# First image's attention: half of the fp16 casts by a converting DMA, and VectorE's other work dealt out one item at a time

## The chip, the cores and the metric

The kernel runs on one core of a Trainium2 chip. A core has a matrix engine (TensorE, PE in the profile, with a row PEld for its weight loads), a vector engine (VectorE, DVE), a scalar engine (ScalarE, ACT), a general engine (GpSimd, POOL), a sync engine (SyncE, SP) that here issues most transfers, and 16 DMA engines that move data. Matrix results land in PSUM, everything else on the core lies in SBUF. Each engine works through its own list of instructions in order, and waits on semaphores for the others.

The metric is the device time of one execution in microseconds; lower is better. The kernel before takes 2591.39 us, the median of three runs (2590.61 to 2596.2).

## What is computed

Two attention layers, one after the other, over x of shape (8, 512, 32, 32): eight images, 512 channels, 1024 positions. The first layer has eight heads of 64 channels and rounds q, k and v to 256 levels; the second has one head of 512 channels. The change touches the first layer's attention only:

```python
def _L0_conv_ref(x, gn_w, gn_b, qkv_w, qkv_b, proj_w, proj_b):
    h = group_norm(x.reshape(b, c, T), gn_w, gn_b)
    qkv = jnp.einsum('oc,bct->bot', qkv_w, h) + qkv_b[None, :, None]
    q, k, v = jnp.split(qkv.reshape(b * NUM_HEADS, -1, T), 3, axis=1)
    q, k, v = fake_quant(q), fake_quant(k), fake_quant(v)
    scale = 1.0 / math.sqrt(math.sqrt(ch))
    w = jnp.einsum('bct,bcs->bts', q * scale, k * scale)
    w = jax.nn.softmax(w, axis=-1)
    a = jnp.einsum('bts,bcs->bct', w, v)
    a = jnp.einsum('oc,bct->bot', proj_w, a) + proj_b[None, :, None]
    return xf + a
...
x = _L0_conv_ref(x, ...)
x = _L1_conv_ref(x, ...)   # group norm, one head of 512 channels, projection, residual
```

## The kernel before

**Stages.** A first phase (to about 590 us) normalises all images and makes q, k and v, which go to DRAM. Then comes the first layer's attention of image 0 (590 to 703 us), interleaved with `fold()`, which multiplies weights of the second layer together. Then two groups of image 1's attention are issued ahead (`LEAD = 2`), image 0 is projected (from 726 us), and from there the second layer of one image and the first layer's attention of the next run side by side to the end.

**Units.** The attention's heads go in pairs (`j`, 0 to 3), the queries in two halves (`hf`) of 512, the keys in eight tiles of 128 (`s`, 0 to 7). One key tile of one half of one pair of one image is a *unit* `u`; an image has 64. A unit goes through these steps:

1. `scores(u)` (line 982): PE makes `st` = k'q for both heads, 128 keys x 2 x 512; ACT takes the exponential to `pt`, fp32, 128x1024 (0.52 MB). `ptp` has four such buffers. On every second unit of image 0, `next(folding)` puts one more product of `fold` ahead of the scores.
2. `split(u)` (line 1010): `pt` is cut into two fp16 tiles whose sum is precise enough: `two[:, 0]` is `pt` cast to fp16 (`cast`), `two[:, 1]` is `pt - two[:, 0]` (`rest`, always on DVE). `partp` has six such buffers. In image 0, units with `s % 4 == 3` are `plain`: they stay fp32, in `aside`, and are not split.
3. `over_keys` (line 1043): PE adds v times both halves to `av`. `totals` (line 1068): PE adds up the exponentials themselves in `sm`.
4. `finish(b, j, hf)` (line 1084), after a half's last unit: ACT copies `av` to `ao` and `sm` to `rs`. After a pair's second half, SP gathers the sums into `apart`; `spread` (DVE) adds and inverts them, writes them to DRAM (`rs_d`), and two transfers broadcast them back into `rs`; `divide` (DVE) multiplies `ao` by `rs`. `rs` has one buffer, which the next pair needs.

Which engine casts, in the kernel before: units with `s % 4 == 2` GpSimd; in image 0 and in the two groups issued ahead, `s == 5` VectorE; all others ScalarE.

**Order of PE's work.** The loop in `attention()` goes by four units. For image 0 (`dense`), with `u` a multiple of four: scores of `u+6`, `u+7`; `over_keys` and `totals` of `u`, `u+1`; split of `u+6`, `u+7`; scores of `u+8`, `u+9`; `over_keys` and `totals` of `u+2`, `u+3`; `finish` after a half's last group; split of `u+8`, `u+9`. At a pair's first group, `load_pair` (line 917) fetches the next pair's q and k into `raw` (two buffers, SP), DVE quantises each (`quant`, `quant2`), and `fetch_v` fetches v into the buffer that comes free and quantises it, with a second copy for the plain tiles (`whole`).

**Who sets the order on the other engines.** `InOrder` wraps DVE, ACT and PE. `dve.later(name, cost, work, ready, within)` and `settle(name)` are a planner for the later images (`InOrder.planned = True`): work is kept in a list with its cost and due time, and put between other work. For image 0 and the two groups issued ahead `planned` is False: `later` runs the work at once, and the framework's scheduler places the instructions of each engine by their dependences. So there each quantisation is issued where `load_pair` stands, and `spread` and `divide` where `finish` stands.

Of the kernel before, what the change touches and what calls it, by code (L numbers as in the profile page):

```python
# [25 lines left out]
PAIRS = HEADS // 2  # L26
# [32 lines left out]
def attn_pair_kernel(  # L59
# [9 lines left out]
    nc = tc.nc  # L69
    PSUM = bass.MemoryType.PSUM  # L70

    class InOrder:
# [73 lines left out]
        def settle(self, what):  # L146

            while True:
                i = next((i for i, c in enumerate(self.chores) if c[0] == what), None)
                if i is None:  # L150
                    return
                self.begin(i)
# [3 lines left out]
    def elements(n):  # L156

        return 0.21 + n * 0.957e-3
# [147 lines left out]
    with ExitStack() as fast:  # L306
# [605 lines left out]
        def plain(b, s):  # L912
            return b == 0 and s % 4 == 3

        ao = {}

        def load_pair(b, j):

            nm = f"{b}_{j}"
            raws = []  # L920

            def fetch(i, src):
                if (b, j, i) == (0, 0, 2):
                    raw = aop.tile([P, NH, 512], F32, tag="ao", name="raw_first").rearrange(
                        "p h n -> p (h n)"
                    )
                else:
                    raw = raw_p.tile([P, T], F32, tag="raw", name=f"raw_{nm}_{i}")
                nc.sync.dma_start(
                    raw if i < 2 else raw.rearrange("p (t d) -> p t d", t=NT), src  # L930
                )
                raws.append(raw)

            def whole(raw, _, i):
                quant2(raw.rearrange("p (t d) -> p t d", t=NT)[:, 3::4, :], vfs[j], i)

            fetch(0, q_d[b][j])
            fetch(1, k_d[b][j])
            qt = qkp.tile([P, T], BF, tag="q", name=f"q_{nm}")
            kt = qkp.tile([P, T], BF, tag="k", name=f"k_{nm}")  # L940
            vt = qkp.tile([P, NT, P], F16, tag="v", name=f"v_{nm}")
            todo = (qt, kt, vt.rearrange("p t d -> p (t d)"))

            if b == 0:
                vfs[j] = xp.tile([P, 2, 256], F32, tag="x", name=f"vf_{nm}")[:, :, 0:P]

            def quants(i):
                for step in (quant, quant2, *([whole] if i == 2 and b == 0 else [])):
                    dve.later(
                        "qk" if i < 2 else "qv", 0.7, lambda step=step: step(raws[i], todo[i], i),  # L950
                        pe.t + 12.0, 45.0,
                    )

            def fetch_v():
                if len(raws) == 2:
                    fetch(2, v_d[b][:, :, bass.ts(j, P)])
                quants(2)

            if (b, j) == (0, 0):
                fetch(2, v_d[b][:, :, bass.ts(j, P)])  # L960
            quants(0)
            quants(1)
            dve.later("qk", 0.0, fetch_v)
            return qt, kt, vt

        settle = dve.settle

        def attention():

# [4 lines left out]
                     for s in range(NT)]  # L974
            pairs = {}
            pairs[0, 0] = load_pair(0, 0)
            pts, parts, avs, sms, rss, ready = {}, {}, {}, {}, {}, {}
            st_free, at_hand = [0.0, 0.0], set()

            aside = l2p.tile([P, 3, NT // 2, 256], F32, tag="vsum", name="aside")  # L980
# [29 lines left out]
            def split(u):  # L1010

                b, j, hf, s = units[u]
                pt, there = pts.pop(u)
                if plain(b, s):
                    parts[u], ready[u] = pt, there
                    return
                two = partp.tile([P, 2, 2, 512], F16, tag="two", name=f"two_{b}_{j}_{hf}_{s}")
                parts[u] = two

                def rest():  # L1020
                    dve.tensor_tensor(two[:, 1], pt, two[:, 0], ALU.subtract)
                    ready[u] = dve.t

                def cast(copy=act.copy):
                    at_hand.add(u)
                    copy(two[:, 0], pt)  # L1026
                    done_at = act.t if copy == act.copy else there + 1.5
                    dve.later("sum", elements(1024), rest, done_at + 0.1, 9.0)

                if s % 4 == 2:  # L1030
                    cast(nc.gpsimd.tensor_copy)
                elif not InOrder.planned and s == 5:
                    cast(dve.tensor_copy)
                else:
                    act.later("cast", 1.02, cast, there, 7.0)

            def need(u):

                while u not in ready:
                    e, name = (act, "cast") if u not in at_hand else (dve, "sum")  # L1040
                    e.begin(next(i for i, c in enumerate(e.chores) if c[0] == name))
# [39 lines left out]
                            mm(row, lhsT=ones16, rhs=two[:, n // 2, n % 2, :], start=(s == 0),  # L1081
                               stop=(s == NT - 1 - (b == 0 and n > 1)))

            def finish(b, j, hf):

                nm = f"{b}_{j}"
                if hf == 0:
                    settle("ao")
                    ao[b, j] = aop.tile([P, NH, 512], F32, tag="ao", name=f"ao_{nm}")
                    rss[b, j] = l1p.tile([P, NH, 512], F32, tag="rs", name=f"rs_{nm}")  # L1090
                aot, rs = ao[b, j], rss[b, j]
                act.do(0.6, lambda: act.copy(aot[:, hf, :], avs.pop((b, j, hf))))
                act.do(0.6, lambda: act.copy(rs[:, hf, :], sms.pop((b, j, hf))))
                if hf == 0:
                    return
                del rss[b, j]
                n = b * PAIRS + j

                apart = small.tile([P, 2, 16], F32, tag="apart", name=f"apart_{nm}")
                for w in range(2):  # L1100
                    nc.sync.dma_start(
                        apart[:, w, :],
                        rs[2 * w * QUAD : 2 * (w + 1) * QUAD : QUAD].rearrange(
                            "r h (p k) -> r h p k", k=16
                        ),
                    )

                def divide():
                    dve.scalar_tensor_tensor(aot, aot, scl[:, 2:3], rs, ALU.mult, ALU.mult)

                def spread():
                    r = rcs[:, n * 16 : (n + 1) * 16]
                    dve.tensor_add(r, apart[:, 0, :], apart[:, 1, :])
                    dve.reciprocal(r, r)
                    nc.sync.dma_start(rs_d[n].rearrange("r (p k) -> (r p) k", k=16), r)
                    for i, r in enumerate(HALF):
                        nc.sync.dma_start(
                            rs[r], rs_d[n][2 * i : 2 * i + 2, :].partition_broadcast(CH)
                        )
                    dve.later("ao", elements(1100), divide, dve.t + 7.0, 20.0)  # L1120

                dve.later("ao", 0.4, spread, pe.t + 5.0, 8.0)

            for u in (0, 2, 4):
                for i in (u, u + 1):
# [3 lines left out]
            for u in range(0, len(units), 4):  # L1129
                b, j, hf, s = units[u]  # L1130
                if hf == 0 and s == 0:
                    n = b * PAIRS + j + 1
                    if n < B * PAIRS:
                        pairs[divmod(n, PAIRS)] = load_pair(*divmod(n, PAIRS))
                    settle("qv")

                def two(what, v):  # L1140
                    if v < len(units):
                        what(v)
                        what(v + 1)

                pe.t += 0.12
                if not late:
                    two(scores, u + 6)
                if late:
                    over_keys((u, u + 1))
                    two(scores, u + 6)  # L1150
                    totals((u, u + 1))
                    over_keys((u + 2, u + 3))
                    totals((u + 2, u + 3))
                    two(split, u + 6)
                    two(scores, u + 8)
                elif dense:
                    over_keys((u, u + 1))
                    totals((u, u + 1))
                    two(split, u + 6)
                    two(scores, u + 8)  # L1160
                    over_keys((u + 2, u + 3))
                    totals((u + 2, u + 3))
                else:
                    over_keys(range(u, u + 4))
                    totals(range(u, u + 4))
                    two(split, u + 6)
                    two(scores, u + 8)
                if s == NT - 4:
                    finish(b, j, hf)
                two(split, u + 8)  # L1170
                pe.t += 0.15
                last = (j, hf, s) == (PAIRS - 1, NH - 1, NT - 4)
                yield b + last
# [989 lines left out]
```

## Time and profile before

| what | before |
|---|---|
| median of three runs | 2591.39 us (2590.61 to 2596.2) |
| the profiled execution's own time | 2596.26 us |
| its span, first to last instruction | 2594.5 us |
| mean granted clock of PE | 0.994 |
| POOL's casts, whole span | 128, 1338 ns mean, 171.3 us |
| DVE's subtractions, whole span | 496, 1235 ns mean, 604.3 us |
| ACT's casts, whole span | 358, 1056 ns mean, 362.6 us |
| image 0's attention, 590 to 703 us: PE, DVE, ACT, POOL busy | 106.48, 100.29, 101.16, 21.00 us |
| the same: DMA share, GB/s | 0.36, 116 |

The profile is of one execution, so its durations add up to its own time, 2596.26 us, and not to the median. Busy times are sums over instructions; a wait is the idle time of an engine ahead of an instruction, with what ended it. The last two rows belong to a window: a stretch of the span with the busy time of every engine inside it, the clock granted to PE and the mean busy share of the 16 DMA engines.

### The profile page before, as it was taken

To read this page: it belongs to the slowest core of one execution; us is meant where nothing else is said; L and a number is where in the kernel's file an instruction comes from. 1 tells how busy PE (TensorE), PEld (TensorE's weight loads), DVE (VectorE), ACT (ScalarE), POOL (GpSimd) and SP (SyncE) were. 2 spreads that over 40 slices of the span, in tenths; PEclk is the share of its full clock that TensorE was granted. 3 is DMA by queue.
4 is the path that set the end of the run, shared out by engine and by line. 5 is a ranking of instruction groups with operands and counts; after the bars stand their busy time and mean duration, and the time that the engine had idled before them with its cause. 6 is when DMAs were issued, how large, how long until landed. Compare 5 with 4: busy or idle time off the path is not lost.

```text
span 2594.5 us, 38713 instructions
## 1 busy us (share of the span) xinstructions
PE 2535.6 (98%) x15670; PEld 1754.2 (68%) x15670; DVE 1905.8 (73%) x2748; ACT 1360.4 (52%) x1696; POOL 193.8 (7%) x153
## 2 busy tenths in 40 slices
PE   7999999999989999999999999999999999999998
PEld 4788888873237765775677577757766775777687
DVE  6788777669867777777877787778777777775544
ACT  3222222218856674666566566647665765664121
POOL 0000000001110001000100011010001000100000
PEclk9899999999999999999999999999999999999999
DMA  4343333334311232223212332231232123212211
GB/s 167 130 148 139 115 119 118 129 126 135 115 50 54 58 111 102 66 78 111 87 56 70 125 99 58 94 107 63 85 107 98 46 79 122 83 51 84 86 37 38
DMA packets 156014, 243.09 MB, mean 94 GB/s; under 512 B 26545, under 2 KB 93105, under 8 KB 154289
## 3 DMA queue, kind: packets, MB, share of 16 engines
q1 hardware_dynamic: 125264, 182.81, 21.3%
q10 hardware_dynamic: 30560, 57.71, 6.5%
q8 instruction: 125, 2.05, 0.3%
q14 instruction: 65, 0.52, 0.1%
HBM read 153.64 MB, written 86.28 MB: 92 GB/s over the span
## 4 chain that ended last, share of the span: by engine, by line
PE 84%; DVE 5%; ACT 2%; issue 2%; DMA 2%; POOL 0%; SPq 0%; ACTq 0%; DVEq 0%
PE s L208 15%; PE o L208 14%; PE qkps L208 12%; PE pj L208 9%; PE av L208 7%; PE v2ps L208 7%; PE g L208 7%; PE vps L208 6%; PE st L208 4%; PE sm L208 3%; DVE two L91 2%; ACT pt L91 1%; DMA rs<-rs_d 0%; DVE acc L91 0%; DVE h L91 0%
## 5 line engine op out<-in xcount | busy, mean ns | idle before, releaser
L91 ACT ACTIVATE pt<-st,esc 128x1024 f32<-128x1024 f32 x496 | 528.6, 1115 | 348.7 <-PE st L208 326.2
L91 DVE TENSOR_TENSOR two<-pt,two 128x1024 f16<-128x1024 f32 x496 | 604.3, 1235 | 129.2 <-POOL two L1026 106.9
L91 ACT CAST two<-pt 128x1024 f16<-128x1024 f32 x358 | 362.6, 1056 | 5.3 <-ACT p L91 5.1
L1026 POOL CAST two<-pt 128x1024 f16<-128x1024 f32 x128 | 171.3, 1338 | 1537.3 <-ACT pt L91 771.5
L208 PE MATMUL av<-two,v 128*32 128x512 f16 x3968 | 244.7, 381 | 0.2
L208 PE MATMUL s<-g,h 128*128 128x256 f32 x1024 | 233.4, 380 | 0.0
L208 PE MATMUL pj<-ao,wp 128*128 128x512 f32 x512 | 223.8, 595 | 0.0
L208 PEld LDWEIGHTS s<-g,h 128*128 128x128 f32 x1024 | 192.9, 190 | 31.0 <-issue 4.3
L91 ACT ACTIVATE u_ring<-qkps,qkbt 128x512 f32<-128x512 f32 x89 | 61.1, 687 | 252.6 <-PE qkps L208 220.3
L208 PE MATMUL st<-q,k 64*128 64x512 bf16 x1024 | 165.8, 383 | 17.6 <-ACT pt L91 12.6
L208 PEld LDWEIGHTS <-v 128*32 128x32 f16 x3968 | 91.3, 96 | 134.0 <-issue 60.7
L208 PE MATMUL s<-g,sums 128*128 128x256 f32 x768 | 178.4, 381 | 0.2 <-DVE p L91 0.2
L208 PEld LDWEIGHTS pj<-ao,wp 128*128 128x128 f32 x512 | 96.0, 190 | 121.6 <-issue 111.1
L208 PE MATMUL o<-p,v 128*128 128x256 f32 x768 | 175.2, 382 | 1.0 <-DVE p L91 1.0
L208 PEld LDWEIGHTS o<-p,v 128*128 128x128 f32 x768 | 144.3, 190 | 27.1 <-issue 5.7
L208 PEld LDWEIGHTS s<-g,sums 128*128 128x128 f32 x768 | 144.7, 190 | 24.2 <-issue 4.1
L208 PEld LDWEIGHTS <-k 64*128 64x128 bf16 x1024 | 35.6, 94 | 156.6 <-issue 155.0
L208 PE MATMUL sm<-two,ones 128*32 128x512 f16 x1984 | 136.1, 379 | 1.9 <-ACT rs L91 1.9
L208 PE MATMUL qkps<-half,w_high 128*128 128x512 f32 x480 | 134.3, 402 | 0.0
L208 PE MATMUL qkps<-half,w_low 128*128 128x512 f32 x480 | 132.3, 398 | 1.9 <-DVE half L91 1.9
L208 PE MATMUL qkps<-half,w_mix 128*128 128x512 f32 x480 | 132.5, 398 | 0.6 <-DVE half L91 0.6
L208 PE MATMUL g<-h,wa 128*128 128x256 f32 x512 | 122.0, 387 | 2.7 <-DVE h L91 2.5
(219 smaller groups left out, 3838.3 us busy)
## 6 DMA issues: line engine op xcount, KB each, us to landing
rs<-rs_d SPq DMA_DIRECT2D x80, 256.0 KB
x<-in_x_dram SPq DMA_DIRECT2D x32, 512.0 KB
q_d<-wa SPq DMA_DIRECT2D x32, 512.0 KB
k_d<-wa SPq DMA_DIRECT2D x32, 512.0 KB
v_d<-v_ring SPq DMA_DIRECT2D x32, 512.0 KB
raw<-q_d SPq DMA_DIRECT2D x32, 512.0 KB
raw<-k_d SPq DMA_DIRECT2D x32, 512.0 KB
x_d<-h SPq DMA_DIRECT2D x64, 256.0 KB
```

What stands on the lines that cost most here:

```text
L91: ins = self.latest = op(*args, **kw).ins
L208: ins = nc.tensor.matmul(ps, lhsT=lhsT, rhs=rhs, **kw).ins
L1026: copy(two[:, 0], pt)
```

## The change

Three parts, all inside the first layer's attention:

- **Casts by DMA.** In image 0 units with `s` in `CAST_BY_DMA = (1, 2, 5, 6)` are cast by `nc.gpsimd.dma_start(two[:, 0], pt)`: a transfer from SBUF to SBUF that reads fp32 and writes fp16, issued by GpSimd. That is 32 transfers. Before, `s` = 1 was ACT's, `s` = 5 DVE's and `s` = 2 and 6 GpSimd's. Units with `s` = 0 and 4 stay on ACT.
- **The subtraction is put off.** For these units `rest` is kept in `put_off` and issued at the split of the unit two later, or when `need(u)` asks for it.
- **Dealing.** In the unplanned part, quantisations, `fetch_v`, `spread` and `divide` go into a list, `dealt`, each with the unit from which it may run (`u + 10` for q, k, `fetch_v` and `spread`, `u + 15` for `divide`, `u + 18` for v, counted from the group at which they are put in). Each split issues at most one of them (`deal`); `settle` issues what has the asked name.

With the branch for `s == 5` gone, units 69 and 77 (image 1, in the groups issued ahead) are cast by ACT instead of DVE.

```diff
--- before.py
+++ after.py
@@ -912,9 +912,26 @@
         def plain(b, s):
             return b == 0 and s % 4 == 3
 
+
+        dealt = []
+
+        def deal(u):
+            i = next((i for i, (at, *_) in enumerate(dealt) if at <= u), None)
+            if i is not None:
+                dealt.pop(i)[2]()
+
+        def settle(what):
+            while True:
+                i = next((i for i, (_, name, _) in enumerate(dealt) if name == what), None)
+                if i is None:
+                    break
+                dealt.pop(i)[2]()
+            dve.settle(what)
+
         ao = {}
-
-        def load_pair(b, j):
+        CAST_BY_DMA = (1, 2, 5, 6)
+
+        def load_pair(b, j, u=None):
 
             nm = f"{b}_{j}"
             raws = []
@@ -946,10 +963,11 @@
 
             def quants(i):
                 for step in (quant, quant2, *([whole] if i == 2 and b == 0 else [])):
-                    dve.later(
-                        "qk" if i < 2 else "qv", 0.7, lambda step=step: step(raws[i], todo[i], i),
-                        pe.t + 12.0, 45.0,
-                    )
+                    name, work = "qk" if i < 2 else "qv", lambda step=step: step(raws[i], todo[i], i)
+                    if u is None or InOrder.planned:
+                        dve.later(name, 0.7, work, pe.t + 12.0, 45.0)
+                    else:
+                        dealt.append((u + (10 if i < 2 else 18), name, work))
 
             def fetch_v():
                 if len(raws) == 2:
@@ -960,10 +978,12 @@
                 fetch(2, v_d[b][:, :, bass.ts(j, P)])
             quants(0)
             quants(1)
-            dve.later("qk", 0.0, fetch_v)
+            if u is None or InOrder.planned:
+                dve.later("qk", 0.0, fetch_v)
+            else:
+                dealt.append((u + 10, "qk", fetch_v))
             return qt, kt, vt
 
-        settle = dve.settle
 
         def attention():
 
@@ -974,7 +994,7 @@
                      for s in range(NT)]
             pairs = {}
             pairs[0, 0] = load_pair(0, 0)
-            pts, parts, avs, sms, rss, ready = {}, {}, {}, {}, {}, {}
+            pts, parts, avs, sms, rss, ready, put_off = {}, {}, {}, {}, {}, {}, {}
             st_free, at_hand = [0.0, 0.0], set()
 
             aside = l2p.tile([P, 3, NT // 2, 256], F32, tag="vsum", name="aside")
@@ -1011,6 +1031,10 @@
 
                 b, j, hf, s = units[u]
                 pt, there = pts.pop(u)
+                if not InOrder.planned:
+                    for v in [v for v in put_off if v < u - 1]:
+                        put_off.pop(v)()
+                    deal(u)
                 if plain(b, s):
                     parts[u], ready[u] = pt, there
                     return
@@ -1021,6 +1045,11 @@
                     dve.tensor_tensor(two[:, 1], pt, two[:, 0], ALU.subtract)
                     ready[u] = dve.t
 
+                if b == 0 and s in CAST_BY_DMA:
+                    nc.gpsimd.dma_start(two[:, 0], pt)
+                    put_off[u] = rest
+                    return
+
                 def cast(copy=act.copy):
                     at_hand.add(u)
                     copy(two[:, 0], pt)
@@ -1029,13 +1058,13 @@
 
                 if s % 4 == 2:
                     cast(nc.gpsimd.tensor_copy)
-                elif not InOrder.planned and s == 5:
-                    cast(dve.tensor_copy)
                 else:
                     act.later("cast", 1.02, cast, there, 7.0)
 
             def need(u):
 
+                if u in put_off:
+                    put_off.pop(u)()
                 while u not in ready:
                     e, name = (act, "cast") if u not in at_hand else (dve, "sum")
                     e.begin(next(i for i, c in enumerate(e.chores) if c[0] == name))
@@ -1081,7 +1110,7 @@
                             mm(row, lhsT=ones16, rhs=two[:, n // 2, n % 2, :], start=(s == 0),
                                stop=(s == NT - 1 - (b == 0 and n > 1)))
 
-            def finish(b, j, hf):
+            def finish(b, j, hf, u):
 
                 nm = f"{b}_{j}"
                 if hf == 0:
@@ -1117,9 +1146,15 @@
                         nc.sync.dma_start(
                             rs[r], rs_d[n][2 * i : 2 * i + 2, :].partition_broadcast(CH)
                         )
-                    dve.later("ao", elements(1100), divide, dve.t + 7.0, 20.0)
-
-                dve.later("ao", 0.4, spread, pe.t + 5.0, 8.0)
+                    if InOrder.planned:
+                        dve.later("ao", elements(1100), divide, dve.t + 7.0, 20.0)
+                    else:
+                        dealt.append((u + 15, "ao", divide))
+
+                if InOrder.planned:
+                    dve.later("ao", 0.4, spread, pe.t + 5.0, 8.0)
+                else:
+                    dealt.append((u + 10, "ao", spread))
 
             for u in (0, 2, 4):
                 for i in (u, u + 1):
@@ -1131,7 +1166,7 @@
                 if hf == 0 and s == 0:
                     n = b * PAIRS + j + 1
                     if n < B * PAIRS:
-                        pairs[divmod(n, PAIRS)] = load_pair(*divmod(n, PAIRS))
+                        pairs[divmod(n, PAIRS)] = load_pair(*divmod(n, PAIRS), u)
                     settle("qv")
 
 
@@ -1166,7 +1201,7 @@
                     two(split, u + 6)
                     two(scores, u + 8)
                 if s == NT - 4:
-                    finish(b, j, hf)
+                    finish(b, j, hf, u)
                 two(split, u + 8)
                 pe.t += 0.15
                 last = (j, hf, s) == (PAIRS - 1, NH - 1, NT - 4)
```

## The prediction

> **What bounds the kernel now.** I read the page's busy shares and slices first, then the windows of the stage, then its timelines by engine.
>
> ```profile
> PE 2535.6 (98%) x15670; PEld 1754.2 (68%) x15670; DVE 1905.8 (73%) x2748; ACT 1360.4 (52%) x1696; POOL 193.8 (7%) x153
> ...
> 600.00:688.00 88.00, 87.92 (x762) 28.04 (x764) 80.00 (x95) 78.76 (x87) 16.88 (x12) 1.00 0.36 115
> 688.00:703.00 15.00, 11.24 (x125) 3.49 (x117) 13.00 (x14) 12.44 (x14) 2.21 (x2) 1.00 0.25 74
> 703.00:726.00 23.00, 17.00 (x196) 5.82 (x195) 19.68 (x21) 22.91 (x25) 7.26 (x4) 1.00 0.31 94
> ```
>
> A window's columns are its width, then busy time of PE, PEld, DVE, ACT, POOL, then the granted clock, DMA share and GB/s. The first image's attention runs from 590 to 703 us: 64 units, a unit being one key tile `s` (0 to 7) of one half of one head pair. Between 600 and 688 PE is busy for 87.92 of 88.00 us, although DVE and ACT are also near nine tenths. A modelled matmul end could hide waits, so I looked at the starts:
>
> ```profile
> 644.61 1.05 PE L208 MATMUL av<-two,v 128*32 128x512 f16 x16
> ...
> 651.89 1.05 PE L208 MATMUL av<-two,v 128*32 128x512 f16 x16
> ...
> 694.98 0.39 PE L208 MATMUL st<-q,k 64*128 64x512 bf16 x2 [0.49 <-ACT pt L91]
> ...
> 702.30 0.61 PE L208 MATMUL sm<-two,ones 128*32 128x512 f16 x8 [1.94 <-ACT rs L91]
> ```
>
> The same group of matmuls recurs every 7.28 us (651.89 − 644.61), four units each, 1.82 us a unit, with no wait shown from 600.75 to 688.67. This holds while the folded weights are computed between the score tiles (`fold`, about 1.06 us every second unit). So here PE bounds, and an easier DVE or ACT can buy nothing. Only at the ends does PE wait: 0.54 and 2.13 us before 600, and about 9.6 us in twelve waits from 688 to 726, nearly all for ACT, with the 1.94 us above the longest. 12.3 us (2.67 + 9.6) is all there is to win.
>
> ```profile
> 645.41 1.04 POOL L1026 CAST two<-pt 128x1024 f16<-128x1024 f32 x1 [6.78 <-ACT pt L91]
> ...
> 643.58 1.22 DVE L91 TENSOR_TENSOR two<-pt,two 128x1024 f16<-128x1024 f32 x1
> ...
> 645.43 2.09 DVE L91 TENSOR_TENSOR two<-pt,two 128x1024 f16<-128x1024 f32 x1
> ...
> 700.30 1.28 DVE L91 SCALAR_TENSOR_TENSOR ao<-ao,scl,rs 128x1024 f32<-128x1024 f32 x1 [1.93 <-DMA rs<-rs_d]
> ...
> 701.66 0.59 ACT L91 COPY rs<-sm 128x512 f32<-128x512 f32 x1 [2.28 <-DVE ao L91]
> ```
>
> A subtraction costs 1.22 us alone and 2.09 beside a POOL cast. The last two lines explain PE's 1.94 us: the division of a pair waits for its sums' broadcast, ACT's copy of the next sums waits for the division (`rs` has one buffer), and PE's `sm` for the copy's bank.
>
> **The change part by part.** *Removed*, in this image: 16 POOL casts (28.3 us over 19 in the window, 1.49 each), 8 casts on DVE (0.69 each, 5.5 us) and 8 on ACT (1.05 each, 8.4 us). DVE's subtractions also lose POOL's company: mean 1375 ns over 62 against about 1210 alone, 10 us. Nearly all of it lies in the stretch where PE has no gap: worth 0 there. Worth something are the cast of unit 1, ahead of unit 2's exponential on ACT (one cast later is 0.95 us, PE's 2.13 us wait shortened), and that of unit 57 (0.95) in the last stretch. PE's own order stays row for row.
>
> *Added*: 32 converting transfers issued by POOL, each 128x1024 f32 read, f16 written. Call L the time from the end of an exponential to the moment when its subtraction can start. The trace has no transfer issued by POOL and none that converts. From below: the smallest landing, 1.39 us. From above: 5.73 us, a load of the same 0.52 MB beside another, plus the longest cast of POOL in the stretch as its issue time, 2.45: 8.2.
>
> ```profile
> 636.24 1.39 DMA rs_d<-rcs
> ...
> 648.88 5.73 DMA raw<-q_d
> ...
> 659.48 4.29 DMA raw<-k_d
> ```
>
> Nearest is a load of the same tile, 4.29 us, plus POOL's shortest row over such a tile (1.04) for the issue: 5.3; units 1 and 2, 5 and 6 come in pairs one exponential (about 1.1 us) apart and a tile occupies all 16 DMA engines for 1.6 us (window 590 to 703: 13.02 MB in 35.8% of 113 us), so the second stands 0.5 behind the first. I take 5.8.
>
> [...]
>
> *Where L counts.* Behind each waiting subtraction DVE holds, in order, the next subtractions, the quantisations (which release `raw` buffers and so SP's loads), the reciprocals (SP's `rs_d` and `rs` transfers behind them) and the division. Four `pt` buffers, which `s` = 3 and 7 do not use, close a loop: an exponential of `s` = 6 (or 2) waits for the subtraction of `s` = 1 (or 5) five units back (1.12 + L + 1.21); one of `s` = 5 (or 1) for that of `s` = 0 (or 4), which stands on DVE behind that of `s` = 6 (or 2), seven units back (1.12 + L + 1.21 + 1.21 and about 1.2 of other DVE work). Twelve units thus need 2L + 7.1, with some 0.1 us for each of four semaphore hops 2L + 7.5. With the folds PE needs 12 x 1.82 = 21.8, so L may be 7.2; without, ACT's pace was 6.2 us in four units, 18.7 for twelve: 5.6.
>
> *The sum at L = 5.8:*
> - Start: −0.95 for the cast of unit 1. Given back: the load `raw_2_1` now stands ahead of unit 5's subtraction on DVE. Its buffer comes free near 601.9 as before, and it lands 4.29 + 1.6 later (it shares the engines with one cast tile), 607.8; subtraction done at 609.0, wanted by PE at 608.8 − 0.95. Wait 1.2, so +0.25 net.
> - 601 to 688: 19.1 < 21.8, cost 0. The cover is PE's own 7.28 us groups: from exponential to `av` a DMA-made unit had 8.9 to 10.4 us and needs 5.8 + 1.2. If the cover is gone (L = 8: 23.5), it costs 1.7 x 4 loops = 7.
> - Units 48 to 58: 19.1 − 18.7, +0.4.
> - The division of pair 2 stands behind unit 58's subtraction on DVE. Unit 58's exponential ended at 694.92, 694.0 at best now; + 5.8 + 1.21 + 1.28 gives 702.3 to 703.2 against 701.58. Its other leg, load, reciprocal and broadcast, shares the engines with the casts: 1.6 later at the load before it, 701.8 + 1.28 = 703.1. Together about +1.5, and late next is PE's `sm`, then every exponential behind it.
> - Casts of units 69 and 77 (second image, s = 5) go from DVE to ACT: ACT is busy 22.91 of 23.00 us there, so 69 costs +0.95; 77 lies under the projection (ACT idle 10.80 us).
> - One transfer in the last stretch that meets a load: +1.6. Over both tails of the pair chain another 0.9 for the same sharing in `apart` and `rs`.
>
> 0.25 + 0 + 0.4 + 1.5 + 0.95 + 2.5 = **+5.6 us**. The quantisation of `v` of pair (1,1) moves behind the projection's first half: 1.5 us of DVE under its gaps of 3.90, 0.62, 0.62 and 0.70 us: 0. POOL's queue holds nothing else in the stage; SP's changes in two places of its order only. The profiled execution took 2596.26 us (span 2594.5), 4.9 above the median 2591.39; the difference is put on the median: 2597.
>
> **The rivals.** *1. Hidden anyway:* with L of 3 to 5 the tile arrives in time everywhere but at the division: 0 to +3, 2593. For it: 10 us between exponential and `av`. Against: POOL must issue, and the DMA engines are already 36% busy.
> *2. The DMA engines become the bound:* if a converted tile takes its engines twice 1.6 us, 32 x 3.2 = 102 us join 41 in a stretch of 113: 143, +30, 2621. It decides from 2.25 us a tile ((113 − 41)/32). Against: the write is half the read.
> *3. Faster:* relief on DVE lets the division go as soon as its broadcast lands, and L near 3. The start gives 0.95, unit 57's cast 0.95, the `sm` wait 1.94, three waits of 0.61: −5.7, 2585.7. Against: ACT gets the cast of unit 69 back, and the division now waits for a transfer.
>
> **How the numbers follow.** Forecast (late tiles, +3 to +18, the upper end L near 8 with the last stretch) 0.48; rival 1 0.28; rival 2 0.14; rival 3 0.10. What a measurement can tell from no change is about 0.2%, 5.2 us. Faster: most of rival 3, 0.09. Same: rival 1, a tenth from the forecast's low end, 0.01 of rival 3: 0.39. Slower: 0.38 + 0.14 = 0.52. The range 2588 to 2622 reaches from rival 3's small half to rival 2's typical value; the forecast's own is 2594 to 2609.
>
> **What would show it.** PE groups at 7.28 us until 688 mean L under 7.2; longer ones with PE waiting for DVE `two` mean L above it. Between an exponential and its subtraction I expect 5.8 us; the `sm` of unit 56 near 704, waiting 2 us or more; the projection starting some 5 us later after the stage's start than 726.0 − 590. DMA share near 0.8 says that the transfers run at the loads' rate; full engines say rival 2. I am wrong if the share of DVE's waits for DMA stays small and the projection starts early.

## The result, and the profile after

The changed kernel takes 2605.14 us, the median of six runs (2602.76 to 2609.14), against 2591.81 us for the kernel before in its six (2590.52 to 2596.2). The medians are 13.3 us apart. The ratio is 1.0047, 95% interval 1.0036 to 1.0057, which makes 12.2 us (9.3 to 14.8); the runs below are compared by their ratios.

The profiled execution took 2609.14 us (span 2607.3 us). From the first exponential of image 0 to the first matmul of its projection, called the stage from here on, it needed 151.3 us instead of 134.9. What lies ahead of the stage was 2.2 us shorter and what lies behind it 1.3 us shorter. Neither can be put down to the change: over the fourteen kernels of this study, which do not differ ahead of the stage, its start moved between 586.5 and 591.5 us, and what lies behind it between 1864.7 and 1868.5 us. So the stage is where to read. First the busy line of the page and the DMA queues of the stage (packets, MB, share of the 16 engines), after the change:

```profile
PE 2540.5 (97%) x15670; PEld 1753.3 (67%) x15670; DVE 1889.8 (72%) x2738; ACT 1355.2 (52%) x1690; POOL 186.9 (7%) x169
```

```profile
q1 hardware_dynamic: 10545, 14.29, 31.6%
q0 software_dynamic: 4608, 8.39, 30.4%
...
two<-pt POOLq DMA_DIRECT2D x32, 256.0 KB, 4.1
```

The new queue q0 holds the 32 transfers: 30.4% of 151 us on all 16 engines, 1.43 us a tile, with a median of 4.1 us from issue to landing. The engines' share has gone from 0.35 to 0.62. Now the stage as one window, before and after, with one short window of it before and five after:

```profile
591.10:726.00 134.90, 122.38 (x1095) 39.08 (x1094) 119.54 (x135) 122.98 (x133) 28.26 (x19) 0.99 0.35 111
...
597.00:600.00 3.00, 3.00 (x7) 0.73 (x6) 3.00 (x4) 2.98 (x5) 1.09 (x1) 0.50 0.84 281
```

```profile
589.00:740.20 151.20, 130.59 (x1095) 40.26 (x1094) 103.18 (x124) 117.60 (x127) 21.80 (x35) 0.93 0.62 151
...
600.00:606.00 6.00, 6.00 (x30) 1.53 (x33) 4.67 (x7) 5.30 (x5) 0.54 (x2) 0.50 0.80 174
650.50:654.00 3.50, 3.32 (x10) 0.84 (x13) 3.24 (x4) 2.82 (x5) 0.53 (x1) 0.53 0.54 101
684.75:688.00 3.25, 3.25 (x16) 0.64 (x19) 2.93 (x4) 3.12 (x5) 0.18 (x1) 0.52 0.72 151
716.00:718.75 2.75, 2.75 (x24) 0.59 (x27) 2.75 (x4) 2.09 (x3) 0.00 (x0) 0.50 0.07 19
732.75:736.00 3.25, 3.25 (x32) 0.76 (x24) 2.27 (x3) 3.25 (x4) 0.00 (x0) 0.50 0.05 8
```

These lines split the 16.3 us. PE ran the same 1095 records, but they took 130.59 us instead of 122.38: 8.2 us more, at a granted clock of 0.93 instead of 0.99. And PE was idle for 20.6 us (151.20 − 130.59) instead of 12.5: 8.1 us more. So half of the loss is waiting, and half is the same matmuls at half speed: the short windows show 0.50 to 0.53 just behind the waits.

The DVE and ACT columns show that the relief came: DVE 16.4 us less busy, ACT 5.4. It bought nothing. Where PE waited, in its timeline and in that of the engines ahead of it (pair 0, and the sums' matmuls of the next two pairs):

```profile
633.99 0.34 SPq L946 DMA_DIRECT2D raw<-k_d  x1
634.38 1.31 SPq L1130 DMA_DIRECT2D apart<-rs  x2
...
641.86 1.16 SPq L1146 DMA_DIRECT2D rs<-rs_d  x2
...
647.67 1.28 DVE L91 SCALAR_TENSOR_TENSOR ao<-ao,scl,rs 128x1024 f32<-128x1024 f32 x1 [4.84 <-DMA rs<-rs_d]
649.03 0.58 ACT L91 COPY rs<-sm 128x512 f32<-128x512 f32 x1 [4.71 <-DVE ao L91]
649.67 0.62 PE L208 MATMUL sm<-two,ones 128*32 128x512 f16 x8 [2.79 <-ACT rs L91]
...
683.14 0.61 PE L208 MATMUL sm<-two,ones 128*32 128x512 f16 x8 [2.15 <-ACT rs L91]
...
715.96 1.04 PE L208 MATMUL sm<-two,ones 128*32 128x512 f16 x8 [4.55 <-ACT rs L91]
```

This is the chain that closes a pair: ACT copies the second half's sums, SP gathers them (`apart`), DVE inverts them, SP writes and broadcasts them (`rs_d`, `rs`), DVE divides, and only then may ACT copy the next sums into `rs` and PE go on with `sm`. Before, the chain took 14.6, 14.7 and 14.0 us (pairs 0, 1, 2; from the end of the copy to the end of the division); after, 18.1, 18.0 and 17.5. Before, PE came to its `sm` 1.16 us after the copy at pair 0 and 0.52 us after it at pair 1, and waited 1.94 at pair 2:

```profile
643.74 0.59 ACT L91 COPY rs<-sm 128x512 f32<-128x512 f32 x1 [0.88 <-DVE ao L91]
...
645.49 0.60 PE L208 MATMUL sm<-two,ones 128*32 128x512 f16 x8
...
673.51 0.59 ACT L91 COPY rs<-sm 128x512 f32<-128x512 f32 x1 [1.52 <-DVE ao L91]
...
674.61 0.60 PE L208 MATMUL sm<-two,ones 128*32 128x512 f16 x8
```

That was all the room there was, and 3.4 us more overran it three times: 9.5 us of waits for `rs` instead of 1.9. Of the growth, 1.5, 1.9 and 2.1 us lie between the copy and DVE's addition, 0.9, 1.3 and 1.1 in the write of the inverted sums, and 1.1, 0.1 and 0.4 in the broadcast.

What DVE waited for in the stage (us in total, times, longest), before and after:

```profile
DVE raw L91 <- DMA raw<-v_d: 4.8, 3, 2.3
DVE ao L91 <- DMA rs<-rs_d: 4.2, 3, 1.9
DVE raw L91 <- DMA raw<-q_d: 3.2, 2, 2.6
...
DVE raw L91 <- DMA raw<-k_d: 1.4, 2, 0.8
```

```profile
DVE two L91 <- DMA two<-pt: 13.3, 8, 4.0
DVE ao L91 <- DMA rs<-rs_d: 12.1, 3, 4.8
DVE raw L91 <- DMA raw<-k_d: 7.1, 4, 2.9
DVE raw L91 <- DMA raw<-q_d: 4.5, 3, 2.7
...
DVE raw L91 <- DMA raw<-v_d: 3.3, 2, 3.0
```

13.6 us of waits for transfers have become 40.3: 13.3 for the new tiles, and 13.4 more for loads and broadcasts that were there before.

### The profile page after: what moved, and what is told of

Same layout as the page of the kernel before. It is cut to its first block, busy times and chain, and to the rows that moved or that the text cites. A ratio compares the mean times of both kernels' runs of the same rounds, so it can differ in the third digit from the quotient of the medians.

```text
span 2607.3 us, 38775 instructions
## 1 busy us (share of the span) xinstructions
PE 2540.5 (97%) x15670; PEld 1753.3 (67%) x15670; DVE 1889.8 (72%) x2738; ACT 1355.2 (52%) x1690; POOL 186.9 (7%) x169
## 4 chain that ended last, share of the span: by engine, by line
PE 84%; issue 5%; DVE 3%; ACT 2%; DMA 1%; POOL 1%; SPq 0%; ACTq 0%; DVEq 0%; POOLq 0%
PE s L208 15%; PE o L208 14%; PE qkps L208 12%; PE pj L208 9%; PE av L208 7%; PE v2ps L208 7%; PE g L208 7%; PE vps L208 6%; PE st L208 4%; PE sm L208 3%; ACT pt L91 1%; POOL two L1049 0%; DVE acc L91 0%; DVE h L91 0%; DVE kept_u L91 0%
## 5 line engine op out<-in xcount | busy, mean ns | idle before, releaser
L91 DVE TENSOR_TENSOR two<-pt,two 128x1024 f16<-128x1024 f32 x496 | 595.0, 1215 | 148.8 <-POOL two L1055 106.3
L91 ACT CAST two<-pt 128x1024 f16<-128x1024 f32 x352 | 356.6, 1056 | 5.3 <-ACT p L91 5.1
L1055 POOL CAST two<-pt 128x1024 f16<-128x1024 f32 x112 | 146.4, 1307 | 1446.5 <-PE sm L208 763.6
L208 PE MATMUL st<-q,k 64*128 64x512 bf16 x1024 | 167.5, 386 | 16.7 <-ACT pt L91 12.2
```

What stands on the lines that cost most here:

```text
L91: ins = self.latest = op(*args, **kw).ins
L208: ins = nc.tensor.matmul(ps, lhsT=lhsT, rhs=rhs, **kw).ins
```

## The experiments

Each is one edit of the changed kernel or of the kernel before. (e1, e3, e7 and e10 also have the branch `s == 5` of before again, so units 69 and 77 go back to DVE in them, as does `s` = 5 where it is not cast by transfer.) "Chain" is the copy-to-division time of pairs 0, 1, 2; "slow PE" is PE's busy time in the stage above the 122.4 us of before.

| run | ratio to before (95%) | stage | PE idle | slow PE | DVE waits for DMA | chain |
|---|---|---|---|---|---|---|
| before | | 134.9 | 12.5 | 0 | 13.6 | 14.6, 14.7, 14.0 |
| changed | 1.0047 (1.0036 to 1.0057) | 151.3 | 20.6 | 8.2 | 40.3 | 18.1, 18.0, 17.5 |
| e1_deal_only | 1.0001 (0.9991 to 1.001) | 136.9 | 12.1 | 2.5 | 13.0 | 14.6, 14.2, 14.7 |
| e2_cast_only | 1.0049 (1.0032 to 1.0066) | 150.8 | 22.9 | 5.5 | 43.4 | 18.4, 15.6, 19.9 |
| e3_two_of_eight | 1.0036 (1.0021 to 1.005) | 146.0 | 21.7 | 1.9 | 33.7 | 16.7, 14.9, 17.5 |
| e4_apart_by_act | 1.006 (1.0043 to 1.0077) | 153.1 | 23.1 | 7.6 | 41.4 | 18.2, 20.5, 16.8 |
| e5_pool_same_order | 1.0049 (1.0032 to 1.0066) | 147.4 | 20.4 | 4.6 | 18.6 | 19.7, 15.5, 16.0 |
| e6_traffic_only | 1.0049 (1.0032 to 1.0066) | 147.1 | 21.0 | 3.7 | 25.4 | 16.9, 16.0, 18.3 |
| e7_hf0_only | 1.0026 (1.0017 to 1.0036) | 144.8 | 18.4 | 4.0 | 26.6 | 15.6, 16.8, 17.0 |
| e8_busy_pe | 1.0038 (1.0024 to 1.0052) | 150.3 | 14.5 | 6.3 | 41.1 | 18.4, 16.8, 14.9 |
| e9_traffic_free | 1.0097 (1.0083 to 1.0112) | 161.4 | 31.3 | 7.7 | 41.3 | 20.9, 19.4, 20.7 |
| e10_two_rs_start | 1.0022 (1.0013 to 1.0031) | 139.9 | 15.5 | 2.1 | 31.3 | 17.8, 18.5, 17.4 |
| e11_two_rs | 1.0031 (1.0019 to 1.0042) | 142.2 | 19.5 | 0.3 | 36.0 | 17.7, 18.4, 18.1 |
| e12_before_two_rs | 0.9999 (0.9991 to 1.0008) | 136.1 | 13.4 | 0.3 | 15.1 | 15.5, 14.3, 14.5 |

(For e8 the 7.1 us of its twelve added matmuls, 0.592 us each, are taken out of "slow PE".) Stage times are of one profile each. "Slow PE" depends on chance by some 3 us, as the last section shows, so the ratios carry the verdicts.

### Which part of the change: e1_deal_only and e2_cast_only

```text
 e1: the branch with dma_start and put_off is taken out;  s == 5 goes back to dve.tensor_copy
 e2: the four calls of dealt.append are taken out;  dve.later everywhere, as before
```

> Every cast goes back to the engine that made it before (units with s = 2 and 6 GpSimd, 5 VectorE, 1 ScalarE) and no subtraction is put off; only the dealing stays. The stage is measured from the first exponential to the projection's first matmul: 134.9 us in the profile before, 151.3 after. Theory 'the transfers': without them the stage is 133 to 137 us and the time within 4 us of before. Rival 'the dealing': the division and the loads stay late without any transfer, the stage is 143 us or more, the sums' matmuls at the pairs' ends wait 2 us or more, and the time is 7 us or more above before.

> The 32 converting transfers and the put-off subtractions stay, the dealing goes: quantisations, spread and division are issued where they were before. Theory 'the transfers': stage 146 to 153 us, time 9 to 15 us above before. Rival 'the dealing': stage at most 139 us, time at most 4 us above before. If each does half, 141 to 145 us and +5 to +8.

Dealing alone made no difference that can be measured (+0.3 us, −2.3 to +2.6); the casts alone lose what the change loses. So the loss comes with the casts by transfer and the put-off subtractions, which e1 takes out together. No run puts the subtractions off and leaves the casts where they were, so what the putting off adds by itself is not tested; e6 below loses as much without it.

### How it grows with their number and place: e3_two_of_eight and e7_hf0_only

```diff
 e3:
-        CAST_BY_DMA = (1, 2, 5, 6)
+        CAST_BY_DMA = (2, 6)
 e7:
-                if b == 0 and s in CAST_BY_DMA:
+                if b == 0 and hf == 0 and j and s in CAST_BY_DMA:
```

> Dealing stays, only s = 2 and 6 are cast by transfer (16 transfers); s = 1 goes back to ScalarE, s = 5 to VectorE. Theory 'the transfers share the 16 DMA engines with the loads and with the pairs' broadcast': half the traffic, about half the loss: stage 140 to 145 us, time +4 to +8. Rival 'the latency of a transfer alone, whatever the number' (every second group still has one in its path): stage 148 us or more, +10 or more. Rival 'only the start and units 1 and 5 are at fault': stage at most 137, within 3 us of before.

> The changed kernel with 12 of the 32 transfers: only in the first half of pairs 1 to 3, away from the stage's start and before the second half, in which a pair's division stands; the other casts as before. Theory 'a late tile costs only where a pair's chain or the start stands behind it on VectorE': stage 135 to 139 us, time within 5 us of before, waits of the sums at most 3 us in one pair. Rival 'every transfer costs its share': 12/32 of 16.4 us is 6.2, stage 141 us or more, time +5 or more.

By the ratios, 12 transfers cost 6.7 us (4.4 to 9.3), 16 cost 9.3 (5.4 to 13.0) and 32 cost 12.2 (9.3 to 14.8). My theory for e7, that transfers far from the start and from the second half are nearly free, fell: they cost 0.56 us each, about as much as those of e3 (0.58). The mean over all 32 is lower (0.38), but the intervals leave room for a cost in proportion to the number, so that halving it saves less than half is not shown.

### Is it SP's queue: e4_apart_by_act

In the timeline above SP's gathering stands behind the load of k, which waits for a `raw` buffer that DVE has still to empty: 3.5 us of the chain at pair 0, 4.0 at pair 2.

```diff
-                    nc.sync.dma_start(
+                    (nc.sync if InOrder.planned else act).dma_start(
                         apart[:, w, :],
```

> The changed kernel with one edit: in the first image's attention and the groups issued ahead ScalarE issues the two gathering transfers of each pair's sums (apart), not SyncE, where they stand behind a load that waits for a raw buffer (3.5 us at the first pair, 4.0 at the third). Theory 'the late division comes from SyncE's queue': the sums' waits of 2.79 and 4.55 us fall below 1 us and the half-clock stretches behind them go, stage 141 to 146 us, time +3 to +7 over before. Rival 'the broadcast is late because the engines are shared, and VectorE's queue': stage 148 us or more, time +10 or more.

ACT issued the gathering 0.03 us after the copy at every pair, and the chain was on the whole no shorter: 18.2, 20.5, 16.8 against 18.1, 18.0, 17.5. The time saved ahead of the gathering was lost behind it, where DVE's addition now came 6.4, 6.9 and 6.3 us after the gathering's issue instead of 3.3, 6.1 and 3.1. The addition stands in DVE's queue behind subtractions and quantisations that wait for their own transfers. My theory fell: as this reads, SP's wait was only the place where DVE's lateness showed.

### Is it the lateness of the tile: e5_pool_same_order

```diff
-                    nc.gpsimd.dma_start(two[:, 0], pt)
+                    nc.gpsimd.tensor_copy(two[:, 0], pt)
```

> The changed kernel with the 32 transfers replaced by casts that GpSimd makes itself (units with s = 1, 2, 5 and 6), subtractions put off and dealing kept as in the change. Theory 'the tile comes late' (a transfer took 3.3 to 10.5 us from exponential to subtraction, a GpSimd cast 1.0 to 2.5 us): stage 133 to 139 us, time within 4 us of before. Rival 'putting the subtraction off and dealing the rest costs it, whoever casts': stage 146 us or more, time +9 or more.

No transfer of a tile, and the same loss (1.0049): the theory as I put it fell, and the numbers are those of its rival, that putting off costs it whoever casts. But the loss is of another kind, so the run does not show the rival either. The tile `two` in the stage, after the change and in this run (duration in ns: least, median, most):

```profile
L91 DVE TENSOR_TENSOR two<-pt,two x45: 1161/1219/1227, 593.9 to 709.7; 128x1024 f16<-128x1024 f32 x45
L1049 POOL DMA_DIRECT2D two<-pt x32: 527/527/1309, 591.3 to 712.6; - x32
```

```profile
L91 DVE TENSOR_TENSOR two<-pt,two x47: 1160/1212/2080, 593.0 to 709.1; 128x1024 f16<-128x1024 f32 x47
L1049 POOL CAST two<-pt x32: 1036/1427/2561, 589.3 to 709.7; 128x1024 f16<-128x1024 f32 x32
```

Here subtractions beside a POOL cast take up to 2.08 us; beside transfers none took over 1.23. DVE is busy for 122.2 us instead of 103.2 and waits 18.6 us for transfers instead of 40.3. (The scheduler also moved at least 16 of DVE's 124 instructions in the stage, so the order is not the change's.) A fuller DVE hurt the pairs' chain here as a waiting one did in the change: PE waited 8.5 us for `rs`, against 9.5.

### Is it the traffic: e6_traffic_only and e9_traffic_free

`spare_d` is a list of 32 tiles in DRAM that nobody reads.

```diff
 e6 (on the kernel before, order of DVE, ACT and SP unchanged):
+                if b == 0 and s in (1, 2, 5, 6):
+                    nc.gpsimd.dma_start(spare_d.pop(), pt)
 e9 (on the kernel before, the same; after each of GpSimd's casts of image 0):
+                    for _ in range(2):
+                        nc.gpsimd.dma_start(spare_d.pop(), q_d[0][0])
```

> The kernel before, every cast where it was, and beside them the change's 32 converting transfers of the same tiles at the same places, into DRAM, where nobody reads the result. It tells the load on the 16 DMA engines from the lateness of the tile. Theory 'the tile comes late': stage 134 to 139 us, time within 4 us of before, though each step of a pair's gathering and broadcast takes up to 1 us longer. Rival 'the shared engines': loads and broadcasts come late all the same, stage 143 us or more, time +6 or more.

> The kernel before, and after each of GpSimd's 16 casts in the first image two converting transfers of a tile's size from DRAM to DRAM, which no buffer and no instruction waits for (in the run with traffic out of the exponentials' tiles, ScalarE waited 4.9 us for such a transfer to let go of a buffer). Theory 'the shared DMA engines': loads and broadcasts come late as there, a pair's chain from the copy of its sums to the end of its division takes 1.5 to 3 us longer than 14.0 to 14.7, stage 141 to 147 us, time +5 to +11. Rival 'the buffers held': stage at most 138 us, time at most +4.

In e6 nobody reads the transfers' results, the order of PE, DVE, ACT and SP is that of before, and the loss is that of the change. So the traffic is enough for a loss of this size, without a late tile and without put-off subtractions. What ACT and DVE waited for in it:

```profile
ACT rs L91 <- DVE ao L91: 11.4, 3, 4.1
ACT pt L91 <- DMA spare_d<-pt: 4.9, 3, 2.5
```

```profile
DVE ao L91 <- DMA rs<-rs_d: 9.5, 3, 3.4
DVE raw L91 <- DMA raw<-v_d: 6.4, 5, 2.4
DVE raw L91 <- DMA raw<-q_d: 5.1, 4, 2.3
DVE raw L91 <- DMA raw<-k_d: 4.4, 3, 2.5
```

DVE's waits for the old loads and broadcasts nearly double, 13.6 to 25.4 us, and the chain grows by 1.3 to 4.3 us. The second ACT line is a flaw: exponentials waited 4.9 us for a transfer that still read their buffer. e9 takes that away, since its transfers read and write DRAM only. There the loss was even 25 us, the DVE waits 41.3 and the chain 19.4 to 20.9:

```profile
DVE ao L91 <- DMA rs<-rs_d: 19.0, 4, 7.0
DVE raw L91 <- DMA raw<-v_d: 13.6, 4, 5.2
```

The sharing theory was right in kind and too small in size. e9 is not the change's load, though: its transfers come in pairs one right behind the other, and they kept the 16 engines for 61 us in all against 46 in the change. So it shows that traffic alone is enough, not how much of the change's loss it is.

### Is it the half clock: e8_busy_pe

```diff
             def totals(us):
                 pe.t += 0.12
+                b, j, hf, s = units[us[0]]
+                if b == 0 and j and hf == 1 and s == 0:
+                    idle = bank(f"idle_{j}")
+                    for i in range(4):
+                        mm(idle, lhsT=wa[:, 0, 0, 0:P], rhs=..., start=(i == 0), stop=(i == 3))
```

> The changed kernel with four fp32 matmuls (128x512, whose result nobody reads) ahead of the sums that wait for a division at pairs 0, 1 and 2, so that TensorE is not idle in most of those waits of 2.79, 2.15 and 4.55 us. Theory 'half of the loss is the half clock that follows a wait': the three stretches at a granted clock of 0.5 behind these waits shrink from 11 us to at most 4, the loss to the clock falls from 9.8 to 4 to 7 us, stage 145 to 149 us, time 2 to 6 us below the changed kernel (+7 to +11 over before). Rival 'the clock falls for another reason, or the matmuls only add': stage 151 us or more, time +13 or more.

The windows around the three places, in which PE now has something to do while it waits:

```profile
644.00:652.00 8.00, 7.39 (x44) 2.66 (x45) 6.07 (x6) 4.92 (x6) 0.53 (x1) 1.00 0.38 73
676.00:684.00 8.00, 8.00 (x54) 2.73 (x56) 6.00 (x6) 4.33 (x6) 0.53 (x1) 1.00 0.46 87
708.00:716.00 8.00, 8.00 (x64) 2.82 (x64) 6.59 (x7) 5.10 (x6) 0.61 (x2) 1.00 0.61 135
```

The clock is 1.00 in all of them, with the chain as late at pair 0 as in the change (18.4 us): there, keeping PE busy kept its clock. At pairs 1 and 2 the chain was shorter in this profile (16.8 and 14.9 us), so less of a wait stood there to be covered. In time the gain is small: 1.0038 against 1.0047, and the intervals overlap. Two stretches at half clock came elsewhere (697.6 and 728.3 us), behind waits that the matmuls did not cover, and the stage was 150.3 us, just above what I expected. The mechanism is shown at one pair of one profile, its worth is not settled.

### Is it the chain: e11_two_rs, e10_two_rs_start, e12_before_two_rs

The pairs 1 and 3 of image 0 keep their sums in `kept_u`, a tile that is idle until the second layer, so the copy of the next sums need not wait for the division. The order of DVE and SP stays as it was.

```diff
-                    rss[b, j] = l1p.tile([P, NH, 512], F32, tag="rs", name=f"rs_{nm}")
+                    rss[b, j] = (
+                        kept_u[:, 0:2].rearrange("p a c n -> p a (c n)") if b == 0 and j % 2
+                        else l1p.tile([P, NH, 512], F32, tag="rs", name=f"rs_{nm}")
+                    )
 e10 has this too:
-                if b == 0 and s in CAST_BY_DMA:
+                if b == 0 and u >= 8 and s in CAST_BY_DMA:
```

> The changed kernel with only the second buffer for the pairs' sums; the order of every engine stays. Theory 'the pairs' chain': the sums' waits (9.5 us in all) and most of the 11 us at half clock behind them go, stage 138 to 143 us, time +2 to +6. Rival 'VectorE waits at the division for the broadcast with the subtractions behind it all the same': the wait moves from the sums to the scores and to the products with v, stage 147 us or more, time +9 or more.

> The changed kernel with a second buffer for the pairs' sums (an idle tile, kept_u, for pairs 1 and 3), so that the copy of a half's sums no longer waits for the division of the pair before, and with the first eight units cast as before. Theory 'the loss is the pairs' chain and the start': stage 134 to 139 us, time within 5 us of before. Rival 'the late tiles hold up VectorE's queue wherever they are, and the exponentials behind it': stage 143 us or more, time +7 or more.

> The kernel before with the same second buffer. Its one long wait for the sums (1.94 us at pair 2) goes: stage 131 to 134.5 us, time 0 to 4 us below before. Rival 'that wait moves to the next exponential': stage 134.5 to 136 us, no change.

PE's waits in e11:

```profile
PE st L208 <- ACT pt L91: 11.0, 15, 1.9
PE av L208 <- DVE two L91: 4.9, 6, 1.1
PE st L208 <- ACT aside L91: 1.8, 3, 0.6
```

The long waits for `rs` are gone and no wait is over 1.91 us. The stage fell from 151.3 to 142.2 us as forecast, with the half clock gone altogether. But the chain itself is as late as in the change (17.7, 18.4, 18.1), and a part of the wait moved, as the rival said: to scores whose exponential waits for a buffer, and to products with v whose subtraction is late. In time that is 1.0031, +8.0 us: about a third of the loss came back (the two intervals overlap a little), and the time missed the theory's +2 to +6. Giving the first eight units their old casts as well (e10) left 1.0022, clear of the change's interval; its +5.7 us just missed what I expected, its stage of 139.9 us as well. These 5.7 us stay: by its waits DVE still loses 31.3 us to transfers. On the kernel before (e12) the second buffer is worth nothing; its one wait of 1.94 us moved to the exponentials. No version here beat the kernel before.

## Why the prediction came out as it did

- **What bounds the stage: right, and read too narrowly.** DVE and ACT were relieved by 16.4 and 5.4 us and the stage gained nothing. But "here PE bounds" hid that PE had only 1.16 and 0.52 us of room ahead of `sm` at pairs 0 and 1. The timeline of before had both numbers; I looked at starts with a wait and not at starts that nearly waited.
- **L, the lateness of a tile: right kind, but one value for a wide spread.** I took 5.8 us. From the exponential's end to the landing it was 4.4 us in the median of the 32, from 3.1 to 8.6, and over 5.8 in eight; the issue came 0.3 us after the exponential and took 0.53 us, not 1.04. DVE stood waiting for a tile eight times: in four the subtraction started 3.2 to 3.7 us after the exponential, in the other four 7.3 to 8.7, and these hold 10.3 of the 13.3 us. In those four the transfer's first packet had itself started 2.3 to 4.4 us after the issue's end, with the 16 engines at 74% or more with other packets, against 0.57 us where they were free. So the late tiles were late by the shared engines too. The times from exponential to subtraction (median 7.2, up to 10.5) are longer by DVE's queue. At 4.4 my sum would have come nearer to rival 1, and been more wrong.
- **The tile's time on the DMA engines: 1.43 us measured, 1.6 taken.** Rival 2 needed 2.25 to decide, and over the stage the engines were 62% busy, not full.
- **"601 to 688 … cost 0": the step that failed.** Its cover, PE's groups with 8.9 to 10.4 us from exponential to `av`, was checked for the tiles and the exponentials' buffers alone. For the tiles it held: PE waited 1.6 us for subtractions in the whole stage. The pairs' chain crosses the same stretch twice, through DVE's and SP's queues, and I priced it only at pair 2 (+1.5) and with 0.9 for sharing. Measured: +3.5, +3.3 and +3.5. The write before the broadcast alone took 0.9 to 1.3 us longer at each pair, and every load that came late held up whatever stood behind it on DVE, whose waits for loads of q, k and v grew from 9.4 to 14.9 us.
- **The half clock: missing from the sum.** The profile before had one such stretch, at 597 us, behind the 2.13 us wait, and I put no price on it. Without it the sum would have had to hold 8.1 us; with it 16.3. For the profiled pair my +5.6 is a third.
- **The start: its first half right.** PE's wait of 2.13 us became 1.18, the forecast 0.95 less. Given back were 0.24, 0.99 and 1.38 us, not 1.2, and a stretch of half clock as well.
- **+1.6 for a transfer that meets a load in the last stretch, +0.4 for units 48 to 58, +0.95 for the cast of unit 69:** not found as such. PE's waits for exponentials were 10.3 us in the whole stage before and 9.3 after. The cast of unit 69 was not tried by itself.
- **The rivals.** Hidden anyway (1) and faster (3) are excluded by the interval. Rival 2 had the right resource and the wrong threshold: e6 and e9 show that shared engines cost here long before they were full on average (they were busy for 0.64 and 0.67 of the stage), since they delayed the loads and the small transfers of a chain without room. The average also hides that the load comes in bunches. The busy tenths of the 16 engines in 40 slices of the stage, before and after:

```profile
DMA  5453000399201350058031050079650500080505
```

```profile
DMA  4998531699996663389378544499957484630004
```

Three slices stood at nine tenths before, ten after. While the chain's write of 8 KB was under way the engines were at 0.08 to 0.09 before, and at 0.62 to 0.71 after.

So the forecast's side and range held, its mechanism (late transfers, then the division, then `sm`) was right, and its size was less than half, for a chain that was priced once instead of three times and a clock that was not priced at all. What stays open is how the loss divides between tiles that come late and loads that come late. DVE's queue adds both up, and e5 and e6 each lose as much as the change with another load on it: the parts do not add. The share of the put-off subtractions is open as well.

## What to carry to other kernels

Before moving work to DMA, look for the chains of small transfers that run beside it, and note how early each one ends, not only where one is waited for: a DMA share of 0.35 left engines free and still no room in a chain with 0.5 us to spare. Read that share by slices, not as an average alone. DVE works its queue in order, so what it waited at the queue's head for a transfer was lost for all that stood behind: relief of 16.4 us was paid with 26.7 us more of waits. And on PE waits cost more than themselves here: the stretches at half clock that followed waits of 1.9 us or more, 3.4 or 6.8 us long, cost another 1.7 or 3.4 us each.

## What the runs showed of the hardware

- **Half clock behind short waits.** Stretches at a granted clock of 0.50 lasted about 3.4 us or 6.8, and once (e9) 10.2. They followed a wait of 1.9 us or more, or several of about 1 us in a row. In the stages of the fourteen profiles each of the 16 waits of 2.39 us or more had one behind it or begun in it; of the 20 waits from 1.91 to 2.20 us ten had. The same first wait of 2.13 us was followed by one in the kernel before, e1, e6 and e7, and not in e3, e9, e10 and e12: chance, as far as the runs show, worth 1.7 us of the stage, which is part of the spread between runs of one kernel. Ahead of the stretches at 600, 651 and 685 us of the changed kernel no wait was longer than 2.79 us.
- **Issue by GpSimd beside a busy DVE.** The issue took 0.53 us in the median of 32, with DVE busy for 68% of the stage, and 1.31 us at most. Taking the queue's packets 128 to a transfer, in 17 of the 32 the first started 0.57 to 0.60 us after the issue's end, in 12 of these with DVE busy for 94% or more of that time; in the 13 that started over 1 us late the 16 engines were at 72% or more with other packets. So in those twelve a busy DVE did not hold the transfer back.
- **A converting transfer** of a 128x1024 tile costs the 16 engines 1.43 us: 128 packets of 2 KB written, 173 ns each in the median. The broadcasts, whose packets of 2 KB are not converted, took 84 ns for one, and the loads, which move 4 KB in a packet, 159. So a packet that reads 4 KB and writes 2 took no less than one that moves 4 KB (173 against 159 ns): the narrower output saved nothing here.
